# One closing pass for the fourth kan of the last two units in place of two

## The chip, the cores and the metric

The kernel runs on one core of one Trainium2 chip. A core has a matrix engine (PE, with its weight loads listed apart as PEld), a vector engine (DVE), an activation engine (ACT), a general engine (POOL), a sync engine that issues transfers (SP), and sixteen DMA engines. Memory on the core is SBUF (128 partitions) and the accumulators of PE (PSUM). Times are microseconds on the device, the median of several runs of the program. All arithmetic is in float32.

## The reference, cut to what matters

The input `x` is (16, 32, 128, 128). Two layers run over it. The first is group norm, an attention over channels, and a residual. The second is group norm and a block of four small networks ("kan") on windows of 8 x 8 pixels, again with a residual:

```
def _fastkan(x, ln_g, ln_b, ws, wb, bb):
    ln = _layernorm(x, ln_g, ln_b)
    basis = jnp.exp(-((ln[..., None] - GRID) / DENOM) ** 2)      # 8 grid points
    flat = basis.reshape(*basis.shape[:-2], -1)
    return flat @ ws.T + jax.nn.silu(x) @ wb.T + bb
...
y = _layernorm(wins, pn_g, pn_b)
a = _fastkan(a from y, k1 ...)          # along one axis of the window
d = _fastkan(d from y, k2 ...)          # along the other
e = _fastkan(y, k3 ...)                 # over the 32 channels
z = a + d + e
z = _fastkan(z, k4 ...)                 # the fourth kan
out = z + wins
```

What matters below: kan 4 of a piece of the image needs the sum of kans 1 to 3 of the same piece. Each kan needs a norm, eight basis functions, eight matrix products and one product with a silu.

## The kernel before, in words

**Units.** The image is cut into N = 64 units. A unit is a tile of 128 partitions x 1024 columns, named by its batch half `bp`, a row block `j` and one of two halves of the channels `kk`. A prologue computes the Gram matrix of each half of the batch, from it the attention as one 256 x 256 matrix, and the parameter tables (`parameters`, lines 539 to 637: the matrices `back`, which spread the norm's factors, the weights `wt_a`, `wt_b`, `ws_a`, `ws_b`, and columns such as `par_a`, `par_b`). It also stores the columns added at the very end in `l0c` (lines 1012 to 1019).

**Passes.** A unit takes an "a" pass (kans 1 and 2, 64 partitions each) and shares a "b" pass. A b pass has 128 partitions too: the weights of kan 3 lie on partitions 0 to 63 of `wt_b` and those of kan 4 on partitions 64 to 127. Pass b of unit n computes kan 3 of unit n and kan 4 of unit n - 2 (`BACK = 2`). Passes b64 and b65, after the last unit, have no unit for kan 3; they compute kan 4 of units 62 and 63, and their other half repeats the same input and is thrown away.

**A pass.** `norm` (line 1193) centres with matmuls on PE, evicts twice and squares on ACT (lines 1203 and 1206), sums the squares on PE (line 1034), takes Ln and Exp on ACT, spreads the factors with `back` on PE (line 1212). `scale` (line 1229, DVE) multiplies. `seed` (lines 1239 to 1247, ACT) makes a basis function by a square and an Exp, and a ratio `up` by an Exp; a b pass has one seed (function 0), an a pass has two (0 and 4). `ladder` (line 1258, DVE) makes each further function from the one before it by a multiplication with the ratio: seven steps with one seed, six with two. `products` (line 1271) begins the accumulation with the silus' matmuls (line 499, called through `direct`), lets POOL write one element (line 1284, an order between two sets of matmuls), and then adds the eight functions, 32 matmuls each (line 479). The silus come from `silus` (line 1149): the silu of unit n together with that of z of unit n - 2 (`LATE = 2`), with a change of the activation table before and back after. In b65 the silu of z(63) precedes the norm of the pass on ACT.

**The end of a unit.** `evict_z` (line 1350) writes z = kans 1 to 3. `result` (line 1493, DVE) adds the accumulator, a column and the tile that `again` (line 1518) reloaded from scratch memory. `store` (line 1504, SP) writes it with eight transfers of 32 partitions x 512 columns, 64 KB each.

**What sets the order.** Each engine executes its instructions in the order in which they are written. A planner (`Flow.run`) chooses it: tasks are Python generators whose steps name an engine, an estimated time and the buffers they take, and the planner follows the lists in `ORDER` per engine. Past the last unit the heads of these lists name work that does not exist, and the planner takes what can start first. Scarce buffers are `u` (6, for basis functions and the norm's square), `X` (2 accumulators of a pass), `Y` (2), `z` (2), `sz` (2, silus of z) and `xh` (2).

Of the kernel before, what the change touches and what calls it, by code (L numbers as in the profile page):

```python
# [19 lines left out]
P = 128  # L20
# [22 lines left out]
SEEDS = {"a": (0, 4), "b": (0,)}  # L43
CLIMB = {"a": (0, 4, 1, 5, 2, 6, 3, 7), "b": tuple(range(NG))}
# [208 lines left out]
def conv_preact_kernel(  # L253
# [87 lines left out]
    par_b = [column() for _ in range(4)]  # L341
    fac_a = const.tile([P, NT], F32, name="fac_a")
# [107 lines left out]
    back = {name: const.tile([P, 4, P], F32, name=f"back_{name}") for name in ("0", "a", "b")}  # L450
    wt_a = const.tile([P, NT, 32], F32, name="wt_a")
    wt_b = const.tile([P, NT, 32], F32, name="wt_b")

# [12 lines left out]
    C_R2, C_XB, C_B, C_BX = range(4)  # L466
    c0w = const.tile([P, NBP, KK, 64], F32, name="c0w")
# [34 lines left out]
    def layers():  # L502
        with ExitStack() as es:
# [35 lines left out]
            def parameters():  # L539
# [3 lines left out]
                back_t = raw[:, 0:384].rearrange("p (k q m) -> p k q m", k=3, q=4)  # L543
# [25 lines left out]
                nc.vector.memset(back_t, 0.0)  # L569
# [6 lines left out]
                for par, top, bottom in (  # L576
                    (par_a, (c1["k1_g"], c1["k1_b"]), (c2["k2_g"], c2["k2_b"])),
                    (par_b, (cr["k3_g"], cr["k3_b"]), (cr["k4_g"], cr["k4_b"])),
                ):
                    g, bp_, *bqs = par  # L580
                    name = "a" if par is par_a else "b"
# [6 lines left out]
                for k, (name, groups, scale) in enumerate(  # L588
# [3 lines left out]
                        ("b", quad, par_b[0]),  # L592
                    )
                ):
                    n, m, own = {"0": (4, 16, own16), "a": (8, 8, own8), "b": (4, 8, own8)}[name]
                    t = back_t[:, k].rearrange("p q m -> p (q m)")
# [35 lines left out]
                TT(wt_b, wt_b, fac_b.unsqueeze(2).to_broadcast([P, NT, 32]), ALU.mult)  # L632
                for k in range(2):
                    yield step("DVE", 0.5)
                    TS(ws_b[:, k, :], st_b[k], fac_b[:, NG:NT], None, ALU.mult)
# [113 lines left out]
            def attention(bp):  # L749
# [271 lines left out]
                if bp == NBP - 1:  # L1021
                    for kind in ("z", "sz", "att", "u"):
                        give(kind)
# [124 lines left out]

            def silus(n):

                y = z = None
                if n < N:
                    y = yield "get", ("yy", n)
                if n >= LATE:
                    z = yield "get", ("z", n - LATE)
                kinds = (["S"] if y is not None else []) + (["sz"] if z is not None else [])
                tiles = yield step("ACT", (4.45 if y is not None else 2.55) + (0.97 if z is not None else 0.0), *kinds)
                wide4 = lambda t: t.rearrange("p l t w -> p (l t w)")
                if y is not None:
                    ACT(wide4(tiles[0]), wide4(y), AF.Silu)  # L1160
                if z is not None:
                    ACT(tiles[-1], z, AF.Silu)
                nc.scalar.preload_act_table_set(TABLES)
                if y is not None:
                    used(("yy", n), "yy", 3)
                    put(("S", n), tiles[0])
                if z is not None:
                    used(("z", n - LATE), "z", 2)
                    put(("sz", n - LATE), tiles[-1])
# [23 lines left out]
            def norm(name, n, wt, rhs, e, then):  # L1193
# [16 lines left out]
                for j in range(4):  # L1210
                    for q in range(4):
                        MM(  # L1212
                            rb[q // 2][:, q % 2, j * P : (j + 1) * P],
                            lhsT=back[name][32 * q : 32 * q + 32, j, :],
# [18 lines left out]
            def seed(name, n, par):  # L1233

                v = yield "get", (name, "scaled", n)
                _, bp_, *bqs = par
                for k, i in enumerate(SEEDS[name]):
                    u, = yield step("ACT", 1.9, "u", lag=0.0)
# [5 lines left out]
                    if k + 1 == len(SEEDS[name]):  # L1244
                        give("yc", LAG)
                    yield step("ACT", 1.81, lag=0.0)
                    ACT(u, u, AF.Exp, scale=-1.0, bias=LIFT[name])  # L1247
                    put(("u", name, n, i), u, LAG)

            def ladder(name, n):  # L1250

                by = yield "get", ("up", name, n)
                for i in CLIMB[name]:
                    if i in SEEDS[name]:
                        continue
# [3 lines left out]
                    used((name, n, i - 1), "u", uses(name, i - 1))  # L1259
# [3 lines left out]
            def uses(name, i):  # L1263
                return 1 + (i + 1 < NG and i + 1 not in SEEDS[name])
# [6 lines left out]
            def products(name, n, wt, also, bank, ws, silus, then, cross):  # L1271
# [14 lines left out]
                for i in CLIMB[name]:  # L1286
# [7 lines left out]
                        i == CLIMB[name][-1],  # L1294
# [4 lines left out]
                    used((name, n, i), "u", uses(name, i))  # L1299
# [65 lines left out]
            def norm_b(n):  # L1365
                y = z = None
                if n < N:
                    y = yield "get", ("yy", n)
                if n >= BACK:
                    z = yield "get", ("z", n - BACK)  # L1370
                parts = lambda t, u: t[:, :, 0, :].rearrange("p h (w u m) -> p u h w m", u=2, m=8)[:, u]
                cols = lambda t, h: t[:, 512 * h : 512 * h + 512]
                two = (y, parts) if n < N else (z, cols), (z, cols) if n >= BACK else (y, parts)

                def then():
                    if n < N:
                        used(("yy", n), "yy", 3)
                    if n >= BACK:
                        used(("z", n - BACK), "z", 2)
# [10 lines left out]
            ticks = {}  # L1390

            def pair_b(n):
# [4 lines left out]
                def bank(acc, at, rows, k, h):  # L1397
                    to = acc[k][at : at + rows, h, :]
                    return to.rearrange("p (h n w) -> p h w n", h=4, w=8) if k else to
# [50 lines left out]
                if n < N:  # L1450
                    t = yield "get", ("S", n)
                if n >= BACK:
                    r = yield "get", ("sz", n - BACK)

                def silus(o, q):
                    k, h = divmod(q, 2)
                    if (r if k else t) is not None:
                        mine = r if k else t
                    else:
                        mine = t if k else r  # L1460
# [178 lines left out]
```

## Time and profile before

| what | us |
|---|---|
| median of three runs (lowest, highest) | 2668.13 (2658.78, 2670.66) |
| the profiled execution, its own time | 2664.4 |
| its span | 2662.6 |
| busy PE / DVE / ACT / POOL | 2532.6 / 2476.4 / 2302.0 / 447.1 |
| z(63) evicted (end of line 1350) | 2608.2 |
| scaling of pass b65 begins | 2620.85 |
| first ladder step of pass b65 | 2628.99 |
| end of the matmuls of pass b65 | 2647.26 |
| last result, last store issued | 2648.73, 2653.35 |

The profile is of one execution, on the clock of its own span. A row of a timeline reads: start, duration, engine, line of the kernel, operation, output and input, how many instructions are merged, and in brackets the idle time of the engine before it with what ended it. A row of a table of windows gives for each engine the busy time in the window with the number of instructions, then the granted share of PE's clock, the mean busy share of the sixteen DMA engines, and what they moved in GB/s.

### The profile page before, as it was taken

The page shows a single profiled execution, that of the slowest core. Times are in us where ns is not written, and L with a number is a line of the kernel's source. Part 1 is how long each engine was busy: PE and PEld are TensorE (multiplying, and loading weights), DVE is VectorE, ACT ScalarE, POOL GpSimd, SP SyncE. Part 2 cuts the span into 40 slices and gives each one's busy share as a digit, 9 for nine tenths or more (in the row PEclk, how much of TensorE's full clock was granted, in tenths as well). Part 3 has the DMA queues.
Part 4 walks back from the last instruction along what each step waited for, and adds up shares of the span by engine and source line. Part 5 has one row for each costly group of instructions (what it writes and reads, how often), then busy time and mean ns, then how long its engine had stood idle before and what let it go on. Part 6 is the DMA issues. An engine that isn't in the chain of part 4 may idle for free.

```text
span 2662.6 us, 126247 instructions
## 1 busy us (share of the span) xinstructions
PE 2532.6 (95%) x57375; PEld 1311.3 (49%) x57375; DVE 2476.4 (93%) x1696; ACT 2302.0 (86%) x1967; POOL 447.1 (17%) x431
## 2 busy tenths in 40 slices
PE   6998999999999999999999999999999999999975
PEld 5884444444444445444444444444444454444432
DVE  4755899999999999999999999999999999999987
ACT  0007699999999999999999999999999999999973
POOL 4300111111111111101111111111111111111100
PEclk9998999999999999999999999999999999999987
DMA  9752345555555554555545555555555555555521
GB/s 239 196 151 65 105 118 146 148 150 146 146 152 148 151 149 137 149 142 147 154 137 149 147 149 152 148 144 146 143 150 147 151 146 152 144 152 149 139 80 40
DMA packets 306614, 379.86 MB, mean 143 GB/s; under 512 B 42913, under 2 KB 240033, under 8 KB 306081
## 3 DMA queue, kind: packets, MB, share of 16 engines
q1 hardware_dynamic: 292864, 352.48, 48.5%
q10 hardware_dynamic: 9504, 16.85, 2.5%
q8 instruction: 453, 7.42, 1.2%
q0 software_dynamic: 3712, 2.46, 0.4%
q14 instruction: 81, 0.66, 0.1%
HBM read 103.18 MB, written 67.11 MB: 64 GB/s over the span
## 4 chain that ended last, share of the span: by engine, by line
PE 36%; ACT 19%; SPq 11%; DMA 9%; DVE 8%; issue 5%; ACTq 0%; DVEq 0%; POOL 0%; POOLq 0%
PE X L479 19%; ACT u L1247 6%; DVE u L1258 5%; ACT u L1239 4%; DMA out<-xh 4%; PE Y L479 4%; PE Y L1034 3%; PE X L499 3%; SPq L1186 3%; SPq L1340 3%; PE Y L1066 2%; SPq L1175 2%; DMA x<-in_x 2%; PE Y L1212 2%; DMA sd<-S 2%
## 5 line engine op out<-in xcount | busy, mean ns | idle before, releaser
L1258 DVE SCALAR_TENSOR_TENSOR u<-R,u 128x2048 f32<-128x2048 f32 x846 | 1904.3, 2287 | 37.6 <-PE X L479 8.5
L479 PE MATMUL X<-u,wt_a 32*32 32x512 f32 x16384 | 669.8, 603 | 7.3 <-DVE u L1258 3.7
L479 PE MATMUL X<-u,wt_b 32*32 32x512 f32 x16896 | 602.2, 603 | 13.1 <-DVE u L1258 12.3
L479 PEld LDWEIGHTS X<-u,wt_a 32*32 32x32 f32 x16384 | 318.5, 103 | 223.9 <-issue 105.1
L1239 ACT ACTIVATE u<-yc,vec 128x2048 f32<-128x2048 f32 x194 | 388.2, 2001 | 33.7 <-DVE yc L1229 21.1
L1247 ACT ACTIVATE u<-u 128x2048 f32<-128x2048 f32 x194 | 368.9, 1902 | 2.0
L1229 DVE TENSOR_TENSOR yc<-yc,Y 128x1024 f32<-128x1024 f32 x260 | 309.9, 1214 | 15.5 <-PE Y L1212 15.4
L479 PEld LDWEIGHTS X<-u,wt_b 32*32 32x32 f32 x16896 | 206.9, 103 | 232.3 <-issue 115.8
L1203 ACT ACTIVATE yc<-Y 128x1024 f32<-128x1024 f32 x260 | 250.0, 1012 | 49.5 <-PE Y L479 49.2
L1284 POOL MEMSET vec<- 128x1 f32 x130 | 12.9, 99 | 1513.6 <-PE X L499 1513.6
L1242 ACT ACTIVATE R<-yc,vec 128x2048 f32<-128x2048 f32 x130 | 258.6, 1989 | 0.0
L1206 ACT ACTIVATE u<-yc 128x2048 f32<-128x2048 f32 x130 | 247.6, 1904 | 2.3 <-ACT yc L1203 0.3
L1066 PE MATMUL Y<-x,pt 128*128 128x512 f32 x512 | 241.6, 615 | 1.3 <-DVE yy L1138 1.3
L1146 POOL TENSOR_SCALAR yy<-yy,vec 128x1024 f32<-128x1024 f32 x64 | 202.6, 3165 | 6.4
L1142 POOL TENSOR_SCALAR yy<-yy,vec,col_r 128x1024 f32<-128x1024 f32 x64 | 171.2, 2676 | 148.8 <-DVE yy L1138 124.1
L736 PE MATMUL X<-R 128*64 128x257 f32 (+3 forms) x2048 | 151.6, 308 | 26.6 <-DVE R L710 26.2
L1066 PEld LDWEIGHTS Y<-x,pt 128*128 128x128 f32 x512 | 93.9, 193 | 148.4 <-issue 145.0
L736 PEld LDWEIGHTS X<-R 128*64 128x64 f32 x2048 | 141.1, 140 | 40.6 <-DVE R L710 28.3
L1327 ACT ACTIVATE ad<-X,col 128x1024 f32<-128x1024 f32 x128 | 135.7, 1120 | 1.6 <-PE X L479 1.6
L499 PE MATMUL X<-sd,ws_a 32*32 32x512 f32 x2048 | 106.4, 605 | 21.8 <-ACT z L1350 18.5
L479 PE MATMUL Y<-yy,c 32*32 32x512 f32 x1056 | 124.6, 597 | 0.0
L1160 ACT ACTIVATE S<-yy 128x2048 f32<-128x2048 f32 x64 | 122.5, 1915 | 0.7
(219 smaller groups left out, 2669.9 us busy)
## 6 DMA issues: line engine op xcount, KB each, us to landing
xh<-xh SPq DMA_DIRECT2D x512, 128.0 KB
d<-yy SPq DMA_DIRECT2D x512, 128.0 KB
sd<-S SPq DMA_DIRECT2D x512, 128.0 KB
ad_r<-ad SPq DMA_DIRECT2D x512, 128.0 KB
x<-in_x SPq DMA_DIRECT2D x256, 128.0 KB
out<-xh SPq DMA_DIRECT2D x512, 64.0 KB
u<-in_x SPq DMA_DIRECT2D x28, 256.0 KB
u<-in_x ACTq DMA_DIRECT2D x28, 256.0 KB
```

What stands on the lines that cost most here:

```text
L479: MM(dst(to, g_), lhsT=wt[32 * g_ : 32 * g_ + 32, :], rhs=rhs(g_, to ^ cross[g_]), start=start, stop=stop,)
L499: done.append(MM(dst(g_ ^ w, q), lhsT=wt[o, q // 2, :], rhs=rhs(o, q), start=start, stop=stop))
L736: MM(g[64 * q : 64 * q + 64, k, lo:hi], lhsT=t[:, b, at : at + 64], rhs=t[:, b, lo:hi], start=first, stop=last,)
L1066: MM(xp[:, u, :], lhsT=pts[bp][:, k, kk * P : (kk + 1) * P], rhs=xr[:, k, u * 512 : (u + 1) * 512], start=k == 0, stop=k == KK - 1,)
L1146: nc.gpsimd.tensor_scalar(turned(yy[:, :, 1, :]), straight(y), unit, zero, ALU.mult, ALU.add)
L1203: ACT(v[:, i * RB : (i + 1) * RB], flat(yt[i]), AF.Identity)
L1206: ACT(sq, v, AF.Square)
L1229: TT(v[:, o], v[:, o], flat(rb[i]), ALU.mult)
L1239: ACT(u, v, AF.Square, bias=bqs[k])
L1242: ACT(up, v, AF.Exp, bias=bp_, scale=2.0)
L1247: ACT(u, u, AF.Exp, scale=-1.0, bias=LIFT[name])
L1258: STT(t, by, BIG, at, ALU.min, ALU.mult)
```

## The change

Pass b64 is gone; the pass with n = N + 1 = 65 (`FINAL`) computes kan 4 of units 62 and 63 together, one in each half. For it there are tables of a third kind "z": `wt_z` and `back["z"]` with kan 4's values on all partitions, and columns `par_z`. Its basis functions climb from two seeds (0 and 4), and the products take them in the order 0, 4, 1, 2, 5, 3, 6, 7. The silus of z(62) and z(63) are made in its `seed`, after the second seed. The results of both units are added together after the pass, and their sixteen stores go out together, for even `b` on SP and for odd `b` on ACT's queue. The rows of unit 62 come out in another order than before, so its reload takes eight transfers of 32 partitions in place of four of 64, and its column comes from a new table `l0z`.

```diff
-SEEDS = {"a": (0, 4), "b": (0,)}
-CLIMB = {"a": (0, 4, 1, 5, 2, 6, 3, 7), "b": tuple(range(NG))}
+SEEDS = {"a": (0, 4), "b": (0,), "z": (0, 4)}
+CLIMB = {"a": (0, 4, 1, 5, 2, 6, 3, 7), "b": tuple(range(NG)), "z": (0, 4, 1, 2, 5, 3, 6, 7)}
...
+    par_z = [column() for _ in range(4)]
...
-    back = {name: const.tile([P, 4, P], F32, name=f"back_{name}") for name in ("0", "a", "b")}
+    back = {name: const.tile([P, 4, P], F32, name=f"back_{name}") for name in ("0", "a", "b", "z")}
+    wt_z = const.tile([P, NT, 32], F32, name="wt_z")
+    l0z = const.tile([P, 2], F32, name="l0z")
...
-                nc.vector.memset(back_t, 0.0)
+                for t in back_t:
+                    nc.vector.memset(t, 0.0)
...
+                    (par_z, (cr["k4_g"], cr["k4_b"]), (cr["k4_g"], cr["k4_b"])),
...
+                        ("z", quad, par_z[0]),
...
                 TT(wt_b, wt_b, fac_b.unsqueeze(2).to_broadcast([P, NT, 32]), ALU.mult)
+                nc.vector.tensor_copy(wt_z[64:P], wt_b[64:P])
+                yield step("POOL", 0.5)
+                nc.gpsimd.dma_start(out=wt_z[0:64], in_=wt_b[64:P])
...
                 if bp == NBP - 1:
+                    for h in range(2):
+                        for b in range(4):
+                            nc.vector.tensor_copy(
+                                l0z[32 * b : 32 * b + 32, h : h + 1],
+                                l0col(bp, KK - 2, C_B)[32 * (b ^ 1 ^ 2 * h) : 32 * (b ^ 1 ^ 2 * h) + 32],
+                            )
...
             def seed(name, n, par):
 
                 v = yield "get", (name, "scaled", n)
-                _, bp_, *bqs = par
-                for k, i in enumerate(SEEDS[name]):
-                    u, = yield step("ACT", 1.9, "u", lag=0.0)
+                kind = form(name, n)
+                _, bp_, *bqs = par_z if kind == "z" else par
+                first = SEEDS[kind][0]
+                for k, i in enumerate(SEEDS[kind]):
+                    if k == 0 or kind != "z":
+                        u, = yield step("ACT", 1.9, "u", lag=0.0)
+                    else:
+                        u = spare
                     ACT(u, v, AF.Square, bias=bqs[k])
...
+                    if k == 0 and kind == "z":
+                        before = yield "get", ("z", N - 2)
+                        end = yield "get", ("z", N - 1)
+                        spare, *to = yield step("ACT", 8.8, "u", "sz", "sz", lag=0.0)
+                    elif kind != "z":
+                        yield step("ACT", 1.81, lag=0.0)
+                    lift = LIFT["b"] + CENTRE[i] ** 2 - CENTRE[first] ** 2 if kind == "z" else LIFT[name]
+                    ACT(u, u, AF.Exp, scale=-1.0, bias=lift)
                     put(("u", name, n, i), u, LAG)
+                if kind == "z":
+                    for k, m in enumerate((N - 2, N - 1)):
+                        ACT(to[k], (before, end)[k], AF.Silu)
+                        used(("z", m), "z", 2)
+                        put(("sz", m), to[k])
...
+            FINAL = N + 1
+
+            def form(name, n):
+                return "z" if (name, n) == ("b", FINAL) else name
...
             def result(n):
+                if n == N - 2:
+                    return
+                todo = []
+                for m in range(n - (n == N - 1), n + 1):
+                    bp, kk, j = units[m]
+                    acc = yield "get", ("last", m)
+                    xh = yield "get", ("again", m)
+                    both_ = [l0z[:, h : h + 1] if m == N - 2 else l0col(bp, kk, C_B + h) for h in range(2)]
+                    todo.append((xh, acc, both_))
+                yield step("DVE", 1.3 * len(todo))
+                for xh, acc, columns in todo:
+                    for h, c in enumerate(columns):
+                        o = slice(512 * h, 512 * h + 512)
+                        STT(xh[:, o], xh[:, o], c, acc[:, h, :], ALU.add, ALU.add)
+                    give("X")
+                put(("result", n), [xh for xh, _, _ in todo])
...
             def store(n):
+                if n == N - 2:
+                    return
+                done = yield "get", ("result", n)
+                yield step("SP", 5.2 * len(done), lag=0.0)
+                for m, xh in zip(range(n + 1 - len(done), n + 1), done):
+                    bp, kk, j = units[m]
+                    for i in range(8):
+                        b, h = i // 2, i % 2
+                        at = j * RB + HALF * h
+                        queue = nc.scalar if n == N - 1 and b % 2 else nc.sync
+                        queue.dma_start(
+                            out=out_rows[bp * KK + kk, b, :, :, at : at + HALF],
+                            in_=xh[32 * (b ^ turn(m, h)) : 32 * (b ^ turn(m, h)) + 32, HALF * h : HALF * h + HALF],
+                        )
...
             def again(n):
...
-                xh, = yield step("SP", 2.6, "xh")
-                for i in range(4):
+                xh, = yield step("SP", 5.2 if n == N - 2 else 2.6, "xh")
+                rows = 64 >> (n == N - 2)
+                for i in range(2 * P // rows):
...
-            both = [("b", n) if b else ("a", n) for n in range(N + BACK) for b in range(2) if b or n < N]
+            both = [("b", n) if b else ("a", n) for n in (*range(N), FINAL) for b in range(2) if b or n < N]
...
-                        every("silus", silus, N + LATE),
+                        every("silus", silus),
```

## The prediction

> **What bounds the kernel now.** I read the page's busy shares first, then its 40 slices, and then, because the change touches only the first 135 us and the last 100 us, the timeline of each engine in the tail and tables of short windows.
>
> ```profile
> PE 2532.6 (95%) x57375; PEld 1311.3 (49%) x57375; DVE 2476.4 (93%) x1696; ACT 2302.0 (86%) x1967; POOL 447.1 (17%) x431
> ...
> PEclk9998999999999999999999999999999999999987
> DMA  9752345555555554555545555555555555555521
> ```
>
> In the body PE, DVE and ACT are all nearly full, so a pass taken out of the body would be worth its engine time. The passes taken out lie in the last two slices, which fill worse. So the tail has to be followed by its chain. DVE in the tail (start, duration, line, operation, output and input, count, idle time before):
>
> ```profile
> 2596.42 2.35 DVE L1229 TENSOR_TENSOR yc<-yc,Y 128x1024 f32<-128x1024 f32 x2
> 2598.68 9.28 DVE L1258 SCALAR_TENSOR_TENSOR u<-R,u 128x2048 f32<-128x2048 f32 x4
> 2607.88 1.40 DVE L1493 SCALAR_TENSOR_TENSOR xh<-xh,l0c,X 128x512 f32<-128x512 f32 x2
> 2609.20 11.73 DVE L1258 SCALAR_TENSOR_TENSOR u<-R,u 128x2048 f32<-128x2048 f32 x5
> 2620.85 2.34 DVE L1229 TENSOR_TENSOR yc<-yc,Y 128x1024 f32<-128x1024 f32 x2
> 2623.11 2.28 DVE L1258 SCALAR_TENSOR_TENSOR u<-R,u 128x2048 f32<-128x2048 f32 x1
> 2627.67 1.41 DVE L1493 SCALAR_TENSOR_TENSOR xh<-xh,l0c,X 128x512 f32<-128x512 f32 x2 [2.28 <-PE X L479]
> 2628.99 16.38 DVE L1258 SCALAR_TENSOR_TENSOR u<-R,u 128x2048 f32<-128x2048 f32 x7
> 2647.32 1.41 DVE L1493 SCALAR_TENSOR_TENSOR xh<-xh,l0c,X 128x512 f32<-128x512 f32 x2 [1.95 <-PE X L479]
> ```
>
> Counting seven ladder steps to a b pass from the end gives the owners. The last x7 is pass 65 (unit 63), the x5, the x1 at 2623.11 and the last of the x4 are pass 64 (unit 62), three of the x4 are pass 63. The three L1493 groups are results 61, 62 and 63. Pass 64 therefore ran mostly inside the time in which pass 65 was being normed. That is the first thing to see: it has cover. PE and ACT in the same stretch:
>
> ```profile
> 2609.16 1.49 PE L499 MATMUL X<-sz,ws_b 32*32 32x512 f32 x32
> 2610.97 4.46 PE L479 MATMUL X<-u,wt_b 32*32 32x512 f32 x128 [0.32 <-POOL vec L1284]
> ...
> 2627.63 3.61 PE L499 MATMUL X<-sz,ws_b 32*32 32x512 f32 x32 [0.17 <-PE X L479]
> 2631.63 6.20 PE L479 MATMUL X<-u,wt_b 32*32 32x512 f32 x128 [0.39 <-POOL vec L1284]
> ...
> 2607.11 1.11 ACT L1350 ACTIVATE z<-X,col_r 128x1024 f32<-128x1024 f32 x1 [2.55 <-PE X L479]
> 2608.24 1.28 ACT L1162 ACT_TABLE_LOAD   x1
> 2609.54 1.06 ACT L1162 ACTIVATE sz<-z 128x1024 f32<-128x1024 f32 x1
> ```
>
> The same PE work costs 1.49 + 4.46 us at 2609 and 3.61 + 6.20 us at 2627, after PE had idled 3.31 us. The clock table explains it (next fence: 0.73 of full in 2622 to 2629). After the last result only stores remain. Columns: span, width, PE, PEld, DVE, ACT, POOL busy, clock, DMA share, GB/s:
>
> ```profile
> 2622.00:2629.00 7.00, 3.52 (x50) 0.46 (x34) 4.72 (x6) 5.69 (x3) 0.00 (x0) 0.73 0.27 75
> ...
> 2650.00:2654.00 4.00, 0.00 (x0) 0.00 (x0) 0.00 (x0) 0.00 (x0) 0.00 (x0) 0.50 0.13 40
> 2654.00:2660.00 6.00, 0.00 (x0) 0.00 (x0) 0.00 (x0) 0.00 (x0) 0.00 (x0) 0.50 0.13 51
> ```
>
> This is the second thing to see. SP issues the eight stores of the last unit from 2648.10 to 2653.35, but the bytes move until about 2660.8. Eight stores of 64 KB wait in the queue and the DMA share stays at 0.13 of 16, that is two engines, at 51 GB/s. The last store is bound by two DMA engines, 11 us for 512 KB.
>
> **The change, part by part.** All sums are against the profiled execution (2664.4 us, span 2662.6); the median of the runs is 2668.13, 3.7 more.
>
> *Pass 64 goes, z(63) comes earlier.* The ladder of pass 63 has pass 64's scaling (2.35 us at 2596.42) in front of its last three steps, and a 0.46 us DVE wait at 2591.82 in which pass 64's square held one of the six u buffers. Without both, z(63) is evicted 2.8 us earlier, at 2605.4 instead of 2608.2. Its other input, the moved-back ad of unit 63, is no obstacle: its issues end at 2598.26, the DMA share is 0.00 in 2600 to 2605, and the copy can start about a microsecond earlier, since evict_a no longer stands behind pass 64's square on ACT.
>
> *Norm of the joint pass.* Today z(63) at 2608.2, a silu with two table loads on ACT (2608.24 to 2611.89), two evictions, a square, sums on PE, Ln and Exp, and the scaling possible at 2619.1: 10.9 us. The silu now lies later, so ACT starts at once after the 1.15 us of matmuls: -2.5 us, 8.4 us. But pass 64's products no longer fill PE between the norm's matmuls; it idles about 4 us. The nearest row of such a start is the 1.96 us that the same broadcast (L1212) took at 2575.80 against 1.17; with the sums that adds about 1.3 us. Scaling starts at 2605.4 + 9.7 = 2615.1. From scaling to the first ladder step it takes 8.1 us today (2620.85 to 2628.99): S = 2623.2, against 2629.0.
>
> *Two seeds, silus behind them.* DVE has six steps instead of seven: -2.3 us for an engine that no longer sets the end. ACT after S: square 2.0, Exp 1.9, a table load 1.28 and two silus at 1.06, so the silus are there at S + 7.2. PE cannot start the products before, for the silus' matmuls open the accumulation; queued behind that wait are all eight groups, and behind those the u buffers: DVE can fill six (two seeds, four steps) and then waits for PE's first group. PE starts after 14 us of idling, so by the slow rows: 3.61 + 0.39 for the silus' matmuls and the hop over POOL, 6.20 for four groups, and four more at 1.1: 14.6 us. The end of the matmuls is S + 22 = 2645.2, against 2647.26 today: **-2.1 us**. Bounds: with PE at full clock throughout (1.49 + 0.32 + 8 x 1.1, and the norm 1.3 faster) -7.4; with z(63) not earlier at all +0.8. I take the slow rows, because every long PE idle in this tail was followed by them.
>
> *Results and stores.* Four L1493 steps in place of two, +1.4 us, but the first store starts after the first pair as before; the others hide behind the stores. Today unit 62's eight stores go out at 2628.44 and drain beneath pass 65's ladder (DMA share 0.13 until 2642); that cover is gone. Now sixteen stores, 1 MB, start together, eight issued by SP and eight by ACT. Issue is not the limit (0.62 us per store against 1.3 us of transfer), so a second issuing queue gains at most a microsecond of the slow start (40 GB/s in 2650 to 2654). No row shows two queues storing 32 rows at once. From below: the two queues use different engines, each drains its 512 KB in the time of today: 0. From above: same two engines at 51 GB/s, 512 KB more: **+10.3 us**. I take the upper value, since eight queued stores of one queue never spread over more than two engines; the choice seems to follow the shape of the transfer (32 rows, in the output as 2 x 16), and that shape is unchanged.
>
> The Trainium skill speaks against this part. "DMA: Bandwidth & Descriptors", section "Issuing engines are not separate DMA queues", says that transfers started from different engines run on the same sixteen DMA engines and only save issue time; its section on the semaphore increment of 16 adds that the outermost size, here 2, limits the engines used and that these are the lowest numbered. The 0.13 share agrees with two engines; that two queues share the two, no row here shows. By the rule this term is +10.3 us, by the lower bound of the trace 0.
>
> *Unit 62's reload* in eight pieces instead of four (+2.4 us of SP issue at 0.6 us each) lies near 2578, over 60 us before its use; the reload of unit 63 waits for store 61's landing (13.8 us after its issue today) and comes near 2623, 20 us before its use. Both cost nothing with that slack; without it each microsecond would count in full.
>
> *The start.* DVE gets, between 104 and 133 us: eight small column operations (0.67 us by those of par_a), one more broadcast and four scalings of the `back` matrix (0.25 + 1.12 us), a copy to wt_z (at most 0.44, the row of L632), three more memsets (about 0.15): 2.5 us, and PE one transpose (0.33). There DVE is busy 26.3 of 29 us and PE 28.0 of 29, and from 133 to 194 PE has no gap at all (61 of 61 us), so little can be won back. Bounds 0 and +3.3 (2.5 plus the semaphore gaps of a few extra steps); I take **+2.0**. The POOL transfer of wt_z comes after POOL's last transfer at 103.9 and waits for DVE; queued behind it is POOL's first normalising operation at 180.5, so it is free; its table is needed 2500 us later. Eight tiny copies for l0z (about 0.8 us, L1018's 0.15 each or less) fall at 325 us, where DVE waits for PE: nothing.
>
> Sum: -2.1 + 10.3 + 2.0 = +10.2 us: 2674.6 against the profiled execution, 2678.3 against the median. I forecast **2678**, which is 0.4% above; under 0.5% (13.3 us) counts as no change here.
>
> **The rivals.**
> 1. *The two queues drain on separate engines.* For it: ACT has no other transfer then. Against: the 0.13 share with eight stores waiting. Store term 0: -2.1 + 2.0, 2668.
> 2. *The removed pass is worth more*, PE stays at full clock: -7.4 instead of -2.1. Against: the 3.61 us row. With shared engines 2673, together with rival 1 2663.
> 3. *Slower, beyond 0.5%:* two queues on two engines disturb each other and the stores run at 40 GB/s throughout, as in 2650 to 2654. 1049 KB then take 26.2 us instead of 11.2: +15.0, in all +14.9: 2683. It decides as soon as the joint rate is under 45 GB/s. Against: one queue reaches 51 after four microseconds.
> That the change saves nothing because pass 64 was covered is already in the forecast.
>
> **How the numbers follow.** Forecast 0.55 (its own range 2673 to 2683; one fifth of it passes 0.5%), rival 1 0.2, rival 2 0.1, rival 3 0.15. Slower 0.11 + 0.11 = 0.22; faster 0.04 (rival 2 with rival 1, helped by the spread of the runs of 12 us); same 0.74. The range goes from 2662 (rivals 1 and 2) to 2687 (rival 3 with the upper ends for the start and z(63)).
>
> **What would show it.** z(63) evicted about 2.8 us earlier relative to the end of a63's ladder; one scaling fewer; silus' matmuls about 7 us after the first ladder step, at 3 to 4 us; a DVE wait for PE before the fifth ladder step; after the last result about 21 to 24 us of stores at DMA share 0.13 and 51 GB/s. A share of 0.26 would mean rival 1, about 40 GB/s rival 3. The prediction is wrong if the order of the body, planned from its start, changes with the longer parameters, for then 60 units shift, not two.

## The result and the profile after

The changed kernel takes 2682.94 us, the median of six runs (2680.47 to 2685.90); the kernel before, in as many runs beside it, takes 2666.30 us (2656.96 to 2670.66). The ratio is 1.0069, with a 95% interval of 1.0048 to 1.0090: slower by 0.7%. The forecast was 2678 us with a range of 2662 to 2687. The time lies in the range; the side it fell on, slower by more than 0.5%, had been given a chance of 0.22 against 0.74 for no change. The profiled execution took 2681.62 us, its span is 2679.8, 17.2 us more than the span before; the medians differ by 16.6. All lines of this section are of the changed kernel unless the text says otherwise.

The page's busy shares, the clock slices and the DMA slices:

```profile
PE 2525.3 (94%) x56992; PEld 1313.3 (49%) x56992; DVE 2458.9 (92%) x1711; ACT 2292.3 (86%) x1958; POOL 449.6 (17%) x431
...
PEclk9998999999999999999999999999999999999986
DMA  9762335555555555555555555555555555555530
```

PE did 7.3 us less work than before, DVE 17.5 us less, ACT 9.7 us less: the pass is gone. The span still grew, so the loss is idle time. The DMA slices, of 67 us each, differ at both ends: the third and the sixth from the left read 6 and 3 instead of 5 and 4, the last two read 3 and 0 instead of 2 and 1. So the start, before 400 us, and the tail are the places to look.

To place it, a common landmark helps. Result 60 is the last result that both kernels make by the same steps. DVE in the tail, from result 60 on (the columns are those of the timelines shown before):

```profile
2575.11 1.41 DVE L1545 SCALAR_TENSOR_TENSOR xh<-xh,l0c,X 128x512 f32<-128x512 f32 x2 [1.41 <-PE X L482]
...
2615.35 1.41 DVE L1545 SCALAR_TENSOR_TENSOR xh<-xh,l0c,X 128x512 f32<-128x512 f32 x2 [1.56 <-PE X L482]
2626.52 2.35 DVE L1245 TENSOR_TENSOR yc<-yc,Y 128x1024 f32<-128x1024 f32 x2 [9.76 <-PE Y L1228]
2634.63 9.02 DVE L1291 SCALAR_TENSOR_TENSOR u<-R,u 128x2048 f32<-128x2048 f32 x4 [5.76 <-ACT u L1274]
2646.41 4.69 DVE L1291 SCALAR_TENSOR_TENSOR u<-R,u 128x2048 f32<-128x2048 f32 x2 [2.76 <-PE X L482]
2653.78 1.41 DVE L1545 SCALAR_TENSOR_TENSOR xh<-xh,l0z,X 128x512 f32<-128x512 f32 x2 [2.68 <-PE X L482]
2655.10 1.40 DVE L1545 SCALAR_TENSOR_TENSOR xh<-xh,l0c,X 128x512 f32<-128x512 f32 x2
```

Before, the same line of result 60 stood at 2564.78:

```profile
2564.78 1.41 DVE L1493 SCALAR_TENSOR_TENSOR xh<-xh,l0c,X 128x512 f32<-128x512 f32 x2 [1.41 <-PE X L479]
```

So 10.3 us are lost before the tail begins. The joint pass itself is there as described: one scaling, six ladder steps, the DVE wait for PE before the fifth. Its silus' matmuls and its eight groups on PE, and the two silus on ACT:

```profile
2640.85 2.96 PE L502 MATMUL X<-sz,ws_b 32*32 32x512 f32 x32 [14.44 <-ACT sz L1278]
2644.21 9.56 PE L482 MATMUL X<-u,wt_z 32*32 32x512 f32 x256 [0.40 <-POOL vec L1317]
```

```profile
2639.74 2.00 ACT L1278 ACTIVATE sz<-z 128x1024 f32<-128x1024 f32 x2
```

The matmuls end at 2653.77, that is 78.7 us after result 60 began, against 82.5 before (2647.26 - 2564.78): 3.8 us gained. Behind them come the stores. The table of windows (span, width, PE, PEld, DVE, ACT, POOL busy, clock, DMA share, GB/s) and the two issuing queues, SP and ACT:

```profile
2658.00:2664.00 6.00, 0.00 (x0) 0.00 (x0) 0.00 (x0) 0.00 (x0) 0.00 (x0) 0.50 0.13 45
2664.00:2670.00 6.00, 0.00 (x0) 0.00 (x0) 0.00 (x0) 0.00 (x0) 0.00 (x0) 0.50 0.13 51
2670.00:2676.00 6.00, 0.00 (x0) 0.00 (x0) 0.00 (x0) 0.00 (x0) 0.00 (x0) 0.50 0.13 51
```

```profile
2654.55 13.66 SPq L1563 DMA_DIRECT2D out<-xh  x8
```

```profile
2654.56 15.47 ACTq L1563 DMA_DIRECT2D out<-xh  x8
```

Two queues issue, and the share is still 0.13, as much as two engines of sixteen that are always busy, at 51 GB/s. From the end of the matmuls to the end of the span it takes 26.0 us, against 15.3 before (2662.6 - 2647.26): 10.7 us lost. The balance of the span: 10.3 - 3.8 + 10.7 = 17.2 us.

What remains is the loss ahead of the tail. It arises near 190 us. PE there, first before, then after; L736 and L747 are the sums of the Gram matrix (the program has 1024 such matmuls for both halves of the batch, and the trace records each as two), and `Y<-d,c` is the centring of the norm of pass a0:

```profile
178.98 15.06 PE L736 MATMUL X<-R 128*64 128x257 f32 x216
194.81 1.86 PE L736 MATMUL X<-R 128*64 128x257 f32 x24 [0.76 <-DVE R L710]
197.22 1.15 PE L479 MATMUL Y<-d,c 32*32 32x512 f32 x32 [0.55 <-DMA d<-yy]
198.31 2.41 PE L736 MATMUL X<-R 128*64 128x257 f32 x32
```

```profile
177.03 11.77 PE L747 MATMUL X<-R 128*64 128x257 f32 x168
195.13 2.02 PE L482 MATMUL Y<-d,c 32*32 32x512 f32 x32 [6.33 <-DMA u<-in_x]
197.08 3.24 PE L747 MATMUL X<-R 128*64 128x257 f32 x32
...
212.28 1.17 PE L1228 MATMUL Y<-lr,back_b 32*128 32x128 f32 x32
213.39 5.16 PE L747 MATMUL X<-R 128*64 128x257 f32 x72
220.78 3.67 PE L1083 MATMUL Y<-x,pt 128*128 128x512 f32 x8 [2.23 <-DVE yc L1245]
```

The norm's matmuls were planned after 972 Gram matmuls and are now planned after 920; in the trace 104 Gram records followed them, and now 208 do. Their tile `d` comes by a transfer; PE could go on at 197.2 before and at 195.1 after, so the tile is not later. (The profile puts this wait down to another transfer, `u<-in_x`; that it is `d` is read from the operands, and from the first experiment below, where the same wait is put down to `d<-yy`.) PE now reaches these matmuls long ahead of the tile, waits 6.33 us, and restarts with 2.02 and 3.24 us for what takes 1.15 and 2.41 without the pause: 6.33 + 0.87 + 0.83, less the 0.76 and 0.55 us that it waited before, are 6.7 us. The clock granted to PE in 150 to 200 us is 0.90 here and was 0.97. Another 1.17 us is a broadcast of pass b0 (`back_b`), which now stands ahead of the last 72 Gram records. The Gram sums end at 218.55 instead of 210.44 (209.67 + 0.77, the row before L1066 in the old trace), and 2.23 us more pass until DVE has freed what the next matmuls need. DVE, which prepares the Gram matrix's inputs, stops behind PE:

```profile
188.45 0.71 DVE L721 STREAM_TRANSPOSE R<-yy 128x512 f32<-128x512 f32 x1
199.16 0.71 DVE L721 STREAM_TRANSPOSE R<-ad 128x512 f32<-128x512 f32 x1 [9.99 <-PE X L747]
```

The Gram sums are late by 8.1 us, the wait for DVE adds 2.23, and the copy of two columns in the attention that follows begins 10.4 us later. Before, then after:

```profile
215.79 0.16 DVE L793 COPY u<-Y 128x2 f32<-128x2 f32 x1 [3.26 <-PE Y L791]
```

```profile
226.16 0.16 DVE L804 COPY u<-Y 128x2 f32<-128x2 f32 x1 [5.53 <-PE Y L802]
```

Result 60 is late by nearly the same amount 2350 us further on. That the two agree to 0.1 us is chance: from the matmuls just ahead of this copy to result 60 the twelve profiled executions of this document take between 2342 and 2356 us. The delay at the start is firmer. In the six executions with the moved order these matmuls begin at 225.7 to 227.8 us and PE waits 6.2 to 7.2 us for `d`; in the six with the old order they begin at 209.3 to 219.3, with a wait of 0.55 to 2.1. Whether the body gives some of it back has to be read from the run times below.

### The profile page after: what moved, and what is told of

The parts are those of the page before. It is cut to its first block, busy times and chain, and to the rows that moved or that the text cites. A ratio compares the mean times of both kernels' runs of the same rounds, so it can differ in the third digit from the quotient of the medians.

```text
span 2679.8 us, 125491 instructions
## 1 busy us (share of the span) xinstructions
PE 2525.3 (94%) x56992; PEld 1313.3 (49%) x56992; DVE 2458.9 (92%) x1711; ACT 2292.3 (86%) x1958; POOL 449.6 (17%) x431
## 4 chain that ended last, share of the span: by engine, by line
PE 37%; ACT 18%; SPq 16%; DMA 14%; DVE 8%; issue 6%; ACTq 0%; DVEq 0%; POOL 0%; POOLq 0%
PE X L482 17%; ACT u L1274 5%; DVE u L1291 4%; DMA x<-in_x 4%; SPq L1202 4%; SPq L1374 4%; SPq L1191 4%; PE X L747 3%; ACT u L1260 3%; DMA out<-xh 3%; PE Y L482 3%; PE X L502 3%; PE Y L1051 3%; SPq L1563 3%; PE Y L1083 3%
## 5 line engine op out<-in xcount | busy, mean ns | idle before, releaser
L482 PE MATMUL X<-u,wt_b 32*32 32x512 f32 x16384 | 581.4, 600 | 1.6 <-DVE u L1291 1.2
L482 PEld LDWEIGHTS X<-u,wt_a 32*32 32x32 f32 x16384 | 321.3, 103 | 225.7 <-issue 105.9
L482 PEld LDWEIGHTS X<-u,wt_b 32*32 32x32 f32 x16384 | 200.4, 103 | 210.2 <-issue 114.0
L747 PE MATMUL X<-R 128*64 128x193 f32 (+3 forms) x2048 | 153.3, 310 | 25.8 <-DVE R L721 24.6
L747 PEld LDWEIGHTS X<-R 128*64 128x64 f32 x2048 | 142.3, 141 | 41.0 <-DVE R L721 26.2
```

The source lines that it names most:

```text
L482: MM(dst(to, g_), lhsT=wt[32 * g_ : 32 * g_ + 32, :], rhs=rhs(g_, to ^ cross[g_]), start=start, stop=stop,)
L747: MM(g[64 * q : 64 * q + 64, k, lo:hi], lhsT=t[:, b, at : at + 64], rhs=t[:, b, lo:hi], start=first, stop=last,)
```

## The experiments

Four claims stood against each other. A: the loss is the planned order at the start, in which PE stands in line behind a late tile, and the stores run on two engines because of the shape of each transfer. B: the added instructions of the start cost it, or the second queue matters for the stores. C: the body makes up what the start loses, or the memory behind the output sets the stores' rate. D: the ladder sets the end of the joint pass, whatever PE does. The interval behind each ratio is the 95% interval. All tails are compared from a landmark (result 60, or the end of the matmuls), because the bodies of two executions of one order differ by some microseconds: with the start's work added and the order kept (`e2_start_work`) result 60 came at 2557.70, 7 us ahead of the kernel before, without a reason in the code.

**The planner's steps alone.** The kernel before, with the steps of the longer `parameters` that name an engine and an estimated time, and not one instruction more:

```diff
                     (par_b, (cr["k3_g"], cr["k3_b"]), (cr["k4_g"], cr["k4_b"])),
...
+                yield step("DVE", 0.8)
...
+                yield step("DVE", 0.2)
+                yield step("PE", 0.4, "Y")
+                yield step("DVE", 1.0)
+                give("Y")
...
+                yield step("POOL", 0.5)
```

> The kernel before with the planner's extra steps at the start alone (0.8 + 0.2 + 1.0 us on DVE, 0.4 on PE, 0.5 on POOL, no instruction added). The first normalising matmuls of unit 0 then stand behind 920 Gram matmuls instead of 972. Theory A (the order costs: PE waits in order for the moved tile of unit 0, with the rest of the Gram sums behind it): +7 to +10 us over before, and the PE wait of about 6 us at 189 to 195 us is seen here too. Theory B (the added instructions cost): 0, within 2 us.

Measured: 2673.17 us against 2659.75 of the kernel before on the same chip, ratio 1.0051 (1.0035 to 1.0068): +13.6 us with no work added (9.3 to 18.1 by the interval), more than the 7 to 10 expected. The trace has the same stop, at the same place in the order (PE of `e1_start_plan`):

```profile
175.69 11.76 PE L742 MATMUL X<-R 128*64 128x257 f32 x168
194.60 2.02 PE L479 MATMUL Y<-d,c 32*32 32x512 f32 x32 [7.15 <-DMA d<-yy]
```

An estimate written for a planner, of work that takes place at 130 us, moved another task at 190 us. This settles A against B for the start.

**The added work alone.** All instructions that the change adds to the start, put into steps that exist already, so that the planner sees no difference:

```diff
-                    yield step("DVE", 0.8)
+                    if name != "z":
+                        yield step("DVE", 0.8)
...
+                    also = [(k, name, scale)] + ([(3, "z", par_z[0])] if name == "b" else [])
...
+                nc.vector.tensor_copy(wt_z[64:P], wt_b[64:P])
+                nc.gpsimd.dma_start(out=wt_z[0:64], in_=wt_b[64:P])
```

> The kernel before with all of the changed kernel's added instructions at the start (columns, broadcast, transpose, four scalings, copy, POOL transfer, eight small copies), put into steps that are there already, so that the planner's times and the order of every other instruction stay as before. Theory A: +1 to +3 us (my term of 2.0 for the start). Theory B: +8 to +11 us. Theory C (what is lost at the start is made up in the body): 0.

Measured: 2661.35 us, ratio 1.0007 (0.9994 to 1.0019), that is +1.9 us with bounds of -1.6 and +5.1. PE waits 1.48 us for `d`, in the old place (PE of `e2_start_work`):

```profile
197.38 1.15 PE L482 MATMUL Y<-d,c 32*32 32x512 f32 x32 [1.48 <-DMA d<-yy]
```

**The whole start, the old tail.** Everything that the change does up to the tables, with both last passes, their results and their stores as before.

```diff
+                    (par_z, (cr["k4_g"], cr["k4_b"]), (cr["k4_g"], cr["k4_b"])),
...
+                        ("z", quad, par_z[0]),
...
+                yield step("POOL", 0.5)
+                nc.gpsimd.dma_start(out=wt_z[0:64], in_=wt_b[64:P])
```

> The whole start of the changed kernel (its added instructions and its planner's steps) with the body and the tail of before. Theories A and B: +10 us, as the shift that the changed kernel shows at 2575 us. Theory C: 0. If it comes out at +16, the tail would cost nothing.

Measured: 2671.30 us, ratio 1.0042 (1.0027 to 1.0058), +11.2 us (7.2 to 15.4). The norm's matmuls wait 6.22 us at 194.12. Steps and instructions together cost no more than the steps alone, and neither here nor in the first run does the body win it back: C falls for the start.

**The change with the old order.** The changed kernel with the start's work in existing steps, as in the second experiment; the tail is the changed one.

```diff
-                    yield step("DVE", 0.8)
+                    if name != "z":
+                        yield step("DVE", 0.8)
...
-                yield step("POOL", 0.5)
                 nc.gpsimd.dma_start(out=wt_z[0:64], in_=wt_b[64:P])
```

> The changed kernel with its added instructions at the start put into existing steps, so that unit 0's first normalising matmuls stand behind 972 Gram matmuls again; the tail is the changed kernel's. Theory A: 7 to 9 us less than the changed kernel, about +8 us over before (tail +6.8, start +1 to +2). Theory B: no gain, +16 us over before.

Measured: 2670.73 us, ratio 1.0037 (1.0024 to 1.0050), +9.8 us against the kernel before (6.4 to 13.3). This is the kernel that the forecast had in fact priced: start +2.0, joint pass -2.1, stores +10.3, sum +10.2. From result 60 to the end it takes 104.5 us, as in the changed kernel (104.7), against 97.8 before and 95.6 to 96.1 in the three experiments above.

**One queue.** The changed kernel with all sixteen last stores issued by SP:

```diff
-                        queue = nc.scalar if n == N - 1 and b % 2 else nc.sync
+                        queue = nc.sync
```

> The changed kernel with all sixteen last stores issued by SP. Theory A (two DMA engines carry all of them, whichever engine issues): the last bytes land at the same time or up to 1.5 us later than in the changed kernel (sixteen issues at 0.62 us are 10 us, still under the 21 us of transfer); DMA share 0.13 and 50 GB/s after the last result, as there. Theory B (the second queue halves the transfer): the changed kernel shows already 0.13, so the two queues would then have been on one engine each; with one queue the rate would fall to 25 GB/s and the end come 20 us later.

Measured: 2682.34 us, ratio 1.0077 (1.0062 to 1.0092). The matmuls end at 2655.2 (2645.01 + 10.21), the span 25.4 us later; with two queues it was 26.0. The queue and a window of `e5_one_queue`:

```profile
2655.99 14.06 SPq L1563 DMA_DIRECT2D out<-xh  x16
```

```profile
2664.00:2670.00 6.00, 0.00 (x0) 0.00 (x0) 0.00 (x0) 0.00 (x0) 0.00 (x0) 0.50 0.13 51
```

As long as the stores keep this shape, the second queue is worth nothing: one queue issues sixteen stores in 14.06 us, two queues need 13.66 and 15.47 for eight each. The Trainium skill, "DMA: Bandwidth & Descriptors", section "Issuing engines are not separate DMA queues", says that the issuing engine only changes the time of issue; share (0.13) and rate (51 GB/s) agree with it here.

**Other pieces, same bytes.** The changed kernel with each of the sixteen last stores cut in two, so that a store covers 16 partitions and its output side begins with 16 instead of 2:

```diff
-                        queue.dma_start(
-                            out=out_rows[bp * KK + kk, b, :, :, at : at + HALF],
-                            in_=xh[32 * (b ^ turn(m, h)) : 32 * (b ^ turn(m, h)) + 32, HALF * h : HALF * h + HALF],
-                        )
+                        for p in range(2) if n == N - 1 else (slice(0, 2),):
+                            rows = 32 * (b ^ turn(m, h)) + (16 * p if n == N - 1 else 0)
+                            queue.dma_start(
+                                out=out_rows[bp * KK + kk, b, p, :, at : at + HALF],
+                                in_=xh[rows : rows + (16 if n == N - 1 else 32), HALF * h : HALF * h + HALF],
+                            )
```

> The changed kernel with each of the last sixteen stores split into two of 16 partitions, whose outermost size is 16 instead of 2; same bytes, same two issuing queues, 32 issues. Theory A (the shape of the transfer holds it on two DMA engines): share well above 0.13 after the last result, limited by issue: sixteen issues per queue at 0.62 us are 10 us, so the end comes 15 us after the end of the matmuls instead of 26: -9 to -11 us against the changed kernel. Theory C (the output memory takes only 50 GB/s at the end): 0.

Measured: 2666.93 us, ratio 1.0012 (0.9995 to 1.0030): 0.57 points or 15 us less than the changed kernel, more than the 9 to 11 us expected. Windows of `e6_spread`:

```profile
2662.00:2664.00 2.00, 0.00 (x0) 0.00 (x0) 1.58 (x3) 0.00 (x0) 0.00 (x0) 1.00 0.50 110
...
2666.00:2668.00 2.00, 0.00 (x0) 0.00 (x0) 0.00 (x0) 0.00 (x0) 0.00 (x0) 0.50 0.60 141
```

The share goes from 0.13 to 0.50 and 0.60, the rate from 51 to 110 and 141 GB/s, and the span ends 11.1 us after the matmuls (2650.67 + 10.19 = 2660.86) instead of 26.0. The memory behind the output took more than twice the rate, so C falls for the stores as well. The same page's section "Why a DMA increments its semaphore by 16 and not by 1" gives the rule: the number of engines is the largest one up to 16 that divides the outermost size of both sides. With 2 it gives two engines, as the 0.13 shows; with 16 all of them, of which the shares 0.50 and 0.60 mean eight to ten busy at a time. The cut changes two things at once, the outermost size and the size of a piece, and no run changes one alone. Against the size of a piece as the cause speaks the kernel before, whose only transfers between 2594 and 2596 are pieces of 128 KB that cover 16 partitions each (`ad_r<-ad`), at a share of 0.81 and 205 GB/s. They stay on the core, so they say nothing of the memory behind the output:

```profile
2594.00:2596.00 2.00, 2.00 (x66) 0.99 (x66) 1.90 (x2) 0.00 (x0) 0.00 (x0) 1.00 0.81 205
```

**Silus in the gap.** The changed kernel with the two silus between the norm's Exp and the seeds, where ACT has nothing to do while DVE scales:

```diff
+                if kind == "z":
+                    yield "get", "normed"
...
+                    to = yield step("ACT", 4.66, "sz", "sz", lag=0.0)
+                    for k, m in enumerate((N - 2, N - 1)):
+                        ACT(to[k], (before, end)[k], AF.Silu)
...
-                        spare, *to = yield step("ACT", 8.8, "u", "sz", "sz", lag=0.0)
+                        spare, = yield step("ACT", 5.7, "u", lag=0.0)
```

> The changed kernel with the two last silus made while ACT is idle between the norm's Exp and the first seed (4.6 us of idle, 4.7 us of work), instead of behind the seeds. Theory A (PE waits for the silus, then starts slow, and DVE waits for PE for buffers): products start 6 us earlier, DVE climbs without its 2.8 us wait, the matmuls end about 16 us after the first ladder step instead of 19: -3 us against the changed kernel. Theory D (the ladder sets the end anyway): 0.

Measured: 2675.94 us, ratio 1.0051 (1.0034 to 1.0068): 0.18 points or 5 us less than the changed kernel, where 3 were expected; the two intervals overlap, so the reading rests on the trace. The timelines of DVE and of PE in `e7_silu_gap`:

```profile
2639.81 13.62 DVE L1296 SCALAR_TENSOR_TENSOR u<-R,u 128x2048 f32<-128x2048 f32 x6 [5.76 <-ACT u L1284]
2654.78 1.41 DVE L1550 SCALAR_TENSOR_TENSOR xh<-xh,l0z,X 128x512 f32<-128x512 f32 x2 [1.35 <-PE X L482]
```

```profile
2631.87 2.96 PE L502 MATMUL X<-sz,ws_b 32*32 32x512 f32 x32 [0.28 <-ACT sz L1260]
```

The silus' matmuls end before the first ladder step begins, the six steps run without a wait, and the matmuls end 14.8 us after that first step instead of 19.1. By these rows PE's wait for the silus cost 4.3 us; without it the ladder does set the end. D is right only for this version, not for the change as made.

**The kernel before with other pieces.** Only the last unit's eight stores of the kernel before, cut in two and put on two queues. All else is the kernel before:

```diff
-                    nc.sync.dma_start(
-                        out=out_rows[bp * KK + kk, b, :, :, at : at + HALF],
...
+                    queue = nc.scalar if n == N - 1 and b % 2 else nc.sync
+                    for p in range(2) if n == N - 1 else (slice(0, 2),):
+                        rows = 32 * (b ^ 2 * h) + (16 * p if n == N - 1 else 0)
+                        queue.dma_start(
+                            out=out_rows[bp * KK + kk, b, p, :, at : at + HALF],
...
```

> The kernel before with the last unit's eight stores split as in the spread run, half on SP and half on ACT. Theory A: the 11 us that its last 512 KB take become 5 us of issue (eight per queue) and a landing: the end comes about 10 us after the end of the matmuls instead of 15.3, -4 to -6 us against before. Theory C: 0.

Measured: 2654.86 us against 2663.19, ratio 0.9975 (0.9964 to 0.9985): 0.25% or 6.7 us below the kernel before, a little more than the 4 to 6 us expected. The last matmuls of `e8_before_spread` end at 2647.95:

```profile
2646.19 1.76 PE L479 MATMUL X<-u,wt_b 32*32 32x512 f32 x32 [1.24 <-DVE u L1258]
```

Its span, 2655.4, ends 7.4 us after them instead of 15.3. The run changes the pieces and the queue together; what cut stores on one queue would take was not run.

**All corrections together, and the same kernel once more.** The first kernel is the changed one with the old order, the cut stores and the silus in the gap (the three diffs above joined); the second is the one just described, on the same chip.

> The joint pass with the three corrections together: the start's added instructions put into steps that exist (the planned order of the body as in the kernel before), the two silus behind the norm's Exp and ahead of the seeds, and the last sixteen stores cut into 16 partitions with 16 as the outermost size. Theory A: from the last result to the end about 11 us, silus' matmuls before the first ladder step is done, matmul end at S + 15; against the changed kernel about -8 to -10 (order), -15 (stores), -4 (silus) minus what of these overlaps: 2655 to 2659 where the kernel before takes 2663, ratio 0.997 to 0.999. The rival (D, the ladder sets the end and the joint pass itself is worth nothing): matmul end no earlier than in the kernel before by its common anchor, result(60), and a time equal to that of the kernel before or above it.

> The kernel before with only unit 63's last eight stores cut into 16 partitions and on two queues, on the same chip as the joint pass with all corrections. Theory A: the end follows the matmul end by 7 to 8 us, ratio to the kernel before 0.9975 again; the joint pass with all corrections ends 2 to 4 us earlier by the tail and loses about 1.5 us at the start, so the two are equal within the runs. Theory D: this one is clearly the fastest, by 3 us or more.

Measured beside the kernel before at 2661.18 us: 2654.32 us with the joint pass, ratio 0.9971 (0.9960 to 0.9982), and 2651.11 us without it, ratio 0.9964 (0.9951 to 0.9977). Result 60 and the last result in both, first `e9_all_kept`, then `e10_before_spread_2`:

```profile
2563.52 1.41 DVE L1552 SCALAR_TENSOR_TENSOR xh<-xh,l0c,X 128x512 f32<-128x512 f32 x2 [1.60 <-PE X L482]
...
2637.97 1.40 DVE L1552 SCALAR_TENSOR_TENSOR xh<-xh,l0c,X 128x512 f32<-128x512 f32 x2
```

```profile
2560.38 1.40 DVE L1493 SCALAR_TENSOR_TENSOR xh<-xh,l0c,X 128x512 f32<-128x512 f32 x2 [1.42 <-PE X L479]
...
2641.13 1.40 DVE L1493 SCALAR_TENSOR_TENSOR xh<-xh,l0c,X 128x512 f32<-128x512 f32 x2 [1.38 <-PE X L479]
```

They lie 0.3% and 0.4% below the kernel before; the intervals of the two overlap. By the trace the tail from result 60 to the end of the span (2647.7 and 2648.5) is 84.2 us with the joint pass and 88.1 without, 3.9 us shorter; the times do not show that gain, and 1.9 us of it would go to the start's added work by the second experiment. Whether one of the two is the faster stays open. By the medians the kernel without the joint pass is 3.2 us the faster; by the ends of the intervals the joint pass, with the order and the stores set right, is at most 4.5 us better than the two passes. What is shown is that the cut stores on two queues are the part that pays.

## Why the prediction was right, and where it was wrong

The time lay in the range and on the slower side, 4.9 us above the forecast. The forecast expected +10.2 us, the span shows +17.2, the medians 16.6. That the range held the time is partly luck: the loss at the start had no term in it, and the time sits at 2683, where rival 3 put it for another reason (stores at 40 GB/s), which the trace refutes. Term by term:

- *The start, forecast +2.0 with bounds of 0 and +3.3, measured +10.3 by result 60.* This is the step that failed. It priced the added instructions, and for these it was right (+1.9 in the run with the instructions alone). It took the order of everything else as given. The forecast did name a changed order as what would make it wrong, but gave that no chance and no price, and spoke of the order of the body. One task moved at the start was enough: 6.33 us of PE with ready Gram matmuls queued behind the wait, 1.7 us of slow restart, and with it every later step of the kernel. The bounds should have had an entry for it, from the 61 us in which the forecast itself had found PE without a gap: there any wait on PE counts in full.
- *The stores, forecast +10.3, measured +10.7.* The upper bound was the right one, for the reason given: the shape of the transfer. Rival 1 (separate engines, share 0.26) and rival 3 (40 GB/s throughout) both fall, by share 0.13 and 51 GB/s. The second queue was to save at most a microsecond; with one queue the stores even ended 0.6 us sooner after the matmuls.
- *The joint pass, forecast -2.1, measured -3.8 in this pair of executions.* The mechanism was right throughout, and the size is less sure than the pair makes it look: from result 60 to the end of the matmuls the old tail takes 80.2 to 82.5 us in its six profiled executions, the changed one 78.3 to 78.7 in four. The gain is then 1.5 to 4.2 us, 2.6 between the means, and the forecast lies inside. In the pair, z(63) came 2.15 us earlier against result 60 (2616.40 - 2575.11 = 41.29 against 43.44), not 2.8. From z(63) to the scaling it took 10.1 us, not 9.7; from the scaling to the first ladder step 8.1, as stated. The DVE wait before the fifth step is there, 2.76 us. The mis-sized part is PE after its pause: the silus' matmuls began 6.2 us after the first ladder step instead of 7.2, as PE starts on the first silu, and they took 2.96 and the eight groups 9.56 instead of 3.61 and 10.6. Together the matmuls ended 19.1 us after that step instead of 22; in two other executions (`e5_one_queue`, `e6_spread`) the eight groups took 10.2 and the matmuls ended 19.8 us after it. Rival 2 (PE at full clock, -7.4) falls: 2.96 us is not 1.49.
- *Unit 62's reload, the transfer of wt_z, the columns of l0z, at nothing.* Nothing in the trace speaks against it: the reload of eight pieces runs from 2589.32 to 2593.58, and the result that needs it is at 2653.78.

The sum of what was priced, tested without the moved task, came out at +9.8 us (6.4 to 13.3) against +10.2. The forecast missed the 0.5% line because one more term existed.

## What to carry to other kernels

Where a planner writes the order, the cost of a change includes what its estimates move elsewhere: compare the order of every engine in the two programs before adding up instructions, and look for a task that now waits for a transfer ahead of ready work on the same engine. Work that ends a kernel has no cover, so removing a covered pass while pushing its stores behind the end exchanges free time for full time. For stores at the end, the shape of each transfer, with the DMA share that it reached, was worth 15 us here and a second issuing queue nothing: read the DMA share after the last result before adding a queue.

## What the runs showed of the hardware that was not expected

- Issue can be held back by the transfers themselves. Eight last stores were issued in 5.25 us before (2648.10 to 2653.35); with a second queue beside it and a DMA share of 0.13 eight took 13.66 us on SP and 15.47 on ACT, and sixteen on SP alone 14.06.
- Cutting 64 KB stores into 32 KB stores, twice as many, made them faster, not slower: 110 to 141 GB/s against 51. Sixteen pieces per queue were issued in 7.6 to 7.9 us.
- How long PE takes to come back after a pause is not a fixed price. After 14.44 us of idling in both, the clock granted to PE stays at 0.50 until 2646 in the changed kernel, 5 us after PE restarts, and until 2648 in `e5_one_queue`, 6 us after; the eight groups take 9.56 and 10.21 us. At the start, 32 matmuls of the norm took 2.02 us after a wait of 2.01 us in `e4_order_kept`, and 1.15 after one of 2.12 in `e8_before_spread`; the clock in 200 to 204 us was 0.63 in the first and 1.00 in the second.
